# A selective-scan kernel: norms' roots on ScalarE, C's products one unit later, and nine of 24 of them on GpSimd instead of six

## The chip, the cores and the metric

The kernel runs on one core of a Trainium2 chip. The metric is the device time of one launch in microseconds (us). Five engines work side by side, each through its own instructions in order: TensorE (PE, with its weight loads PEld), VectorE (DVE), ScalarE (ACT), GpSimd (POOL) and SyncE (SP), which here only issues DMAs. An instruction waits on semaphores for what it reads, and everything behind it on its engine waits with it.

## The reference

Two layers over an image tensor `x` of 8 x 96 x 64 x 64 (float32), seen as 8 sequences of 4096 tokens with 96 channels.

Layer 0 is a selective state-space block on the group-normalised input, with 192 inner channels and 16 states:

```python
xz = u @ in_proj_w.T;  xm, z = split(xz)
xm = silu(causal_depthwise_conv4(xm) + conv_b)
dt, Bm, Cm = split(xm @ x_proj_w.T)            # 6, 16, 16
delta = softplus(dt @ dt_proj_w.T + dt_proj_b)
A = -exp(A_log)
# for each token t, channel e, state n:
h = exp(delta * A) * h + delta * Bm * xm
y = sum_n h * Cm + xm * D
out = layer_norm((y * silu(z)) @ out_proj_w.T) * ln_gamma + ln_beta
x = x + out
```

Layer 1 adds linear attention without softmax (`q k^T / 4` applied to `v`, all of it linear) on a layer norm of `x`, and then a feed-forward part on a second layer norm, whose products are rounded to an 8-bit format (5 exponent bits, 2 mantissa bits) and whose sums are rounded to 16 bits, with a relu between. Both layer norms and the one in layer 0 need, for each token, `(v - mean) / sqrt(var + 1e-5)`.

## The kernel before

**Chunks and units.** Two batch elements are worked together (a pair p; there are 4 pairs), and 4096 tokens are cut into 8 chunks c of T = 512, so 32 chunks follow each other. In a chunk the state `h` has 192 channels x 16 states x 2 batch elements = 6144 rows, that is 24 units of 128 partitions x 2 x 512. Unit u stands for a channel block j = u // 8 (NJ = 3), a group of four states g = (u // 2) % 4 and a batch element b = u % 2 (`where`). The partitions of a unit are 4 states x 32 channels, its two halves h are two channel blocks.

**One unit** (`unit`, L711):

- GpSimd multiplies `du` (delta times xm) by the rows of B, into `dbu` (`products_b`, L659), AHEAD = 3 units early, into AHEAD + 1 = 4 buffers.
- ScalarE takes `da = exp(delta * A)` (`decay`, L681) into two PSUM banks, for unit u + 1, each half right behind the scan that frees its bank.
- VectorE runs two scans (L741), one for each half, that read `da` from PSUM and `dbu` from SBUF and write `hs` (3 buffers). Their initial state is the last column of the same unit in the chunk before, copied by ScalarE (L719, L722) into `state`.
- `hs` is multiplied by C. For most units VectorE does it (L763), with C broadcast over partitions into a PSUM bank `cc` by a matmul (`rows_c`, L671). For the units in POOLED = (4, 5, 12, 13, 20, 21) GpSimd does it (`pooled`, L770), with C read from an SBUF tile `c` that DMAs filled with rows broadcast over 32 partitions (`rows`, L643).
- PE sums the products over the states of a pair of units into `y` (`sums`, L695). At the end of each j, `gate` (L709, VectorE) multiplies by silu(z), and `skip` (L703) starts the next `y` with xm * D.

Note on `sums` in `unit`: it is called at even u for the pair that ended at u - 1 unless that unit is in POOLED, and for a pooled pair three units after it, at u = 8 and 16. For the pair (20, 21) that call would fall on u = 24, which does not exist, so the pair is not summed.

**The other work** is cut into generator steps and spread over the units by hand in the table STEPS: `P` (`chain_p`: normalise, convolve, project, Silu, Softplus for the chunk after next), `E` (`chain_e`: output projection, norms, Gram matrix of the chunk before), `F0` and `F1` (`chain_f`: attention and feed-forward of the chunk 9 places back, one batch element each, so from chunk 9 on), `G` (group-norm statistics) and `W` (attention weights). In a row such as `"3: F1 F0 P | F1 G6"` the names left of the bar are taken before the unit's scans, those right of it after them; `*` starts a chain. SyncE's queue holds the chunk's loads in the order in which they are issued: at the end of a chunk B's rows (units 16, 18, 20, 22) and C's rows (unit 23) for the next chunk, in unit 0 eight loads of 256 KB (`spread`, L634: `du` and `dl`, delta), then the store `t1d` (L883, last step of E) and in unit 2 the load `xr` (L822).

**Norms** (`norm_stats`, L395 on): VectorE takes statistics (L406, L408). The rest (`ends`: scale the mean by -1, add eps, raise to the power -0.5, multiply; L412, L131, L132, L414) goes to GpSimd and is put off with `later("norms", ...)` until the next unit's `now("norms")`, or until `normalise` (L420, ScalarE) settles it. There are two norms of 8 columns in E and one of 4 columns in each F chain, so four a chunk.

**ScalarE's tables.** Silu, Softplus and Exp need different function tables; the compiled kernel loads them where the function changes (ACT_TABLE_LOAD).

**Casts.** In an F chain the three relu results are cast to 8 bits by GpSimd (L1011), put off with `later("others", ...)` and settled before the w2 matmul (L1033), which is F1's step in unit 3's front and F0's in unit 15's. The step behind it reads the result on ScalarE (L1038, L1042).

## Time and profile before

Times of three runs: 3162.42, 3166.31 and 3171.55 us, the median 3166.31. The profiled execution is known by its span of 3160.5 us, from its first to its last instruction; its own time is not listed apart from the three.

| what | value |
|---|---|
| time, median of three runs | 3166.31 us |
| span of the profiled execution | 3160.5 us |
| VectorE busy | 2935.2 us, 93% |
| GpSimd busy | 2840.7 us, 90% |
| TensorE busy | 2469.6 us, 78%, mean granted clock 0.807 |
| ScalarE busy | 2263.9 us, 72% |
| DMA engines busy | 57% (mean 140 GB/s) |

How it is read: "busy" is the time in which an engine works on an instruction; waiting, and the issuing of DMAs, does not count. A row of the costliest groups gives line, engine, operation, what it writes and reads, shapes, count, busy time, mean duration in ns, and behind the bar the idle time of the engine just before these instructions with what ended most of it. A row of the timeline gives start and duration in us, engine, line and operation; rows of one line that follow each other are merged (x2), and a bracket tells an idle time and its releaser. SPq is SyncE's queue, and a DMA is there only by its issue; "DMA to landing" is the time from issue to arrival.

The first scans of successive chunks start 82 to 96 us apart in the timeline: about 88 us in chunks 1 to 8, and about 94 in the chunks after, which also run F.

### The profile page before, as it was taken

What the parts mean: (1) busy time and instruction counts of PE and PEld (TensorE: products, weight loads), DVE (VectorE), ACT (ScalarE), POOL (GpSimd) and SP (SyncE); (2) the same over time, 40 slices, a digit from 0 to 9 for tenths busy, and PEclk for the clock granted to TensorE, in tenths of its full rate; (3) what the DMA queues carried; (4) which work ended last, traced back from release to release, by engine and by line L of the source; (5) the groups of instructions that cost most, each with busy time, mean ns of one, the idle gap of its engine ahead of it and who ended that gap; (6) DMA issues with size and microseconds to landing.
All of it is one profiled execution on the core that took longest, in us unless ns stands there. A gap on an engine that the chain in (4) does not pass through costs nothing. (4 is left out here: it accounts for less than half of the span.)

```text
span 3160.5 us, 35127 instructions
## 1 busy us (share of the span) xinstructions
PE 2469.6 (78%) x9450; PEld 928.7 (29%) x9450; DVE 2935.2 (93%) x4265; ACT 2263.9 (72%) x4360; POOL 2840.7 (90%) x1921
## 2 busy tenths in 40 slices
PE   6787787878787777777777778777888778887777
PEld 2122222222222223222233323222323222332344
DVE  4999999999999999999999999999999999999945
ACT  3666666667677777777777777777877777777656
POOL 2999999999999999999999999999999999999955
PEclk8677777787778888888888877898888888877668
DMA  6655556665555667555667555567565466755322
GB/s 149 152 122 137 134 156 152 160 150 135 141 143 135 138 162 175 146 129 125 141 164 170 141 146 125 137 157 170 146 148 127 124 144 162 169 132 134 95 70 73
DMA packets 253037, 443.75 MB, mean 140 GB/s; under 512 B 37605, under 2 KB 45990, under 8 KB 252838
## 3 DMA queue, kind: packets, MB, share of 16 engines
q1 hardware_dynamic: 247846, 439.40, 56.9%
q10 hardware_dynamic: 4992, 2.11, 0.3%
q8 instruction: 74, 1.21, 0.2%
q14 instruction: 125, 1.02, 0.1%
HBM read 349.11 MB, written 92.27 MB: 140 GB/s over the span
## 5 line engine op out<-in xcount | busy, mean ns | idle before, releaser
L659 POOL TENSOR_TENSOR dbu<-du,b 128x1024 f32<-128x1024 f32 x768 | 1804.6, 2371 | 112.6 <-DVE hs L741 65.5
L741 DVE TENSOR_TENSOR_SCAN hs<-da,state,dbu 128x512 f32<-128x512 f32 x1290 | 1573.5, 1265 | 25.6 <-ACT da L681 24.6
L681 ACT ACTIVATE da<-dl,aneg 128x512 f32<-128x512 f32 x1474 | 1000.6, 688 | 665.4 <-DVE hs L741 644.2
L763 DVE TENSOR_TENSOR pr<-hs,cc 128x1024 f32<-128x1024 f32 x576 | 698.7, 1213 | 35.1 <-DVE hs L741 0.5
L695 PE MATMUL y<-pr,ssum 128*32 128x512 f32 x2816 | 585.1, 831 | 113.3 <-DVE pr L763 113.3
L770 POOL TENSOR_TENSOR pr<-hs,c 128x1024 f32<-128x1024 f32 x192 | 453.8, 2363 | 36.6 <-DVE hs L741 30.4
L459 PE MATMUL mp<-u,wk 96*64 96x512 f32 x1488 | 398.1, 658 | 66.6 <-ACT xm L477 66.4
L671 PE MATMUL cc<-cs,sel 64*128 64x512 f32 x576 | 330.0, 583 | 144.8 <-DVE pr L763 144.4
L671 PEld LDWEIGHTS cc<-cs,sel 64*128 64x128 f32 x576 | 121.6, 215 | 557.3 <-DVE pr L763 296.8
L741 DVE TENSOR_TENSOR_SCAN hs<-da,dbu 128x512 f32<-128x512 f32 x184 | 213.2, 1205 | 17.4 <-POOL dbu L659 9.9
L516 PE MATMUL mp<-dbl,dtT 12*128 12x512 f32 x186 | 158.9, 947 | 56.8 <-ACT cs L506 38.5
L695 PEld LDWEIGHTS y<-pr,ssum 128*32 128x32 f32 x2816 | 87.9, 132 | 380.6 <-DVE pr L763 201.6
L791 PE MATMUL mE<-woT,zs 128*128 128x192 f32 x744 | 146.6, 350 | 66.7 <-ACT t1e L799 45.1
L459 PEld LDWEIGHTS mp<-u,wk 96*64 96x64 f32 x1488 | 97.0, 145 | 293.6 <-issue 156.6
L132 POOL TENSOR_TENSOR rs<-rs,mhalf 128x8 f32<-128x8 f32 (+1 forms) x128 | 173.3, 1354 | 10.7
L791 PEld LDWEIGHTS mE<-woT,zs 128*128 128x128 f32 x744 | 127.3, 200 | 126.8 <-ACT t1e L799 70.5
L703 PE MATMUL y<-xm,dd 128*128 128x512 f32 x192 | 129.2, 760 | 22.4 <-DVE zs L709 21.9
L467 PE MATMUL mp<-u,wz 96*64 96x512 f32 x372 | 137.0, 825 | 4.3 <-ACT xm L485 4.3
L1011 POOL CAST h<-h 128x512 fp8e5<-128x512 f16 x192 | 117.6, 622 | 24.8 <-DVE h L1003 15.8
L719 ACT COPY state<-hs 128x2 f32<-128x2 f32 x736 | 130.1, 181 | 0.2
L420 ACT ACTIVATE o<-x,nm,rs 128x96 f32<-128x96 f32 x256 | 98.6, 455 | 36.4 <-POOL nm L414 34.4
L531 POOL TENSOR_TENSOR du<-delta,xm 128x512 f32<-128x512 f32 x93 | 117.1, 1273 | 0.0
(306 smaller groups left out, 3234.1 us busy)
## 6 DMA issues: line engine op xcount, KB each, us to landing
du<-lu SPq DMA_DIRECT2D x380, 256.0 KB, 5.5
dl<-ld SPq DMA_DIRECT2D x380, 256.0 KB, 7.9
b<-bd SPq DMA_DIRECT2D x512, 128.0 KB, 5.0
lu<-du SPq DMA_DIRECT2D x96, 256.0 KB, 5.7
ld<-delta SPq DMA_DIRECT2D x93, 256.0 KB, 2.4
c<-bd SPq DMA_DIRECT2D x128, 128.0 KB, 4.4
xg<-in_x_dram SPq DMA_DIRECT2D x32, 384.0 KB, 3.8
xr<-in_x_dram SPq DMA_DIRECT2D x32, 384.0 KB, 8.7
```

Source lines behind the costliest of these rows:

```text
L132: nc.gpsimd.tensor_tensor(out_, out_, mhalf[0 : out_.shape[0], 0 : out_.shape[1]], op=ALU.pow)
L459: nc.tensor.matmul(ps[64 * b : 64 * b + 64, :], lhsT=wk[:, k, 64 * j : 64 * j + 64], rhs=u[:, b, k : k + T], start=(k == 0), stop=(k == 3),)
L467: nc.tensor.matmul(ps[64 * b : 64 * b + 64, :], lhsT=wz[:, 64 * j : 64 * j + 64], rhs=u[:, b, 3 : T + 3], start=True, stop=True,)
L516: nc.tensor.matmul(ps, lhsT=dtT[:, j, :], rhs=dbl[0 : 2 * RANK, :], start=True, stop=True)
L659: nc.gpsimd.tensor_mul(dbu, s["du", j][:, 2 * b : 2 * b + 2, :], s["b", g][:, b, :].unsqueeze(1).to_broadcast([128, 2, T]),)
L671: nc.tensor.matmul(cc, lhsT=sel[64:128, g, b], rhs=s["cs"][64:128, :], start=True, stop=True)
L681: nc.scalar.activation(da, s["dl", j][:, 2 * b + h, :], AF.Exp, scale=aneg[:, 2 * j + h, g : g + 1])
L695: nc.tensor.matmul(s["y"][q : q + 32, :], lhsT=ssum, rhs=pr[:, h, :], start=False, stop=(g == NG - 1),)
L741: nc.vector.tensor_tensor_scan(hs[:, h, :], s.pop(("da", u, h)), dbu[:, h, :], 0.0 if first else state["last"][:, u, h : h + 1], ALU.mult, ...
L763: nc.vector.tensor_mul(pr, hs, s.pop(("cc", u)).unsqueeze(1).to_broadcast([128, 2, T]))
L770: nc.gpsimd.tensor_mul(pr, s["hs", u], s["c", g][:, b, :].unsqueeze(1).to_broadcast([128, 2, T]))
L791: nc.tensor.matmul(ps[:, 2 * k * C : 2 * (k + 1) * C], lhsT=zs[:, j, tok : tok + 128], rhs=woT[:, j].rearrange("p b c -> p (b c)"), start= ...
```

## The change

- The root of a norm: ScalarE takes Ln of the variance plus eps and then Exp of -0.5 times it (`power`, in the "norms" list). VectorE multiplies -mean by the result in one instruction (`shift`, in a new list "shifts" that is worked off after the first scan of a unit). GpSimd's four instructions a norm go. The group norm's own root stays on GpSimd.
- `exp_and_ln` loads, by name, a table set with exp and ln right behind each Silu and Softplus.
- `times_c`: VectorE's product with C for unit u - 1 stands between the two scans of unit u. `rows_c` stands behind the scans. `sums` is called at odd u for the pair that ended at u - 2, for every pair, so also (20, 21). `pr` has 3 buffers for 4.
- POOLED = (1, 4, 6) counts within each eight units, so nine of 24 products are GpSimd's. C's rows for these three places are loaded by twelve DMAs of 64 KB, four for each place (`rows_pooled`), in unit 1 of the chunk itself; before, four DMAs of 128 KB brought both places of group 2 in unit 23 of the chunk before.
- In STEPS one step of F0 (its four normalisations) goes from unit 3's front to unit 4's end.

```diff
-POOLED = (4, 5, 12, 13, 20, 21)
-POOLED_G = 2
+POOLED = (1, 4, 6)
...
-    3: "F1 F0 P | F1 G6",
-    4: "| E",
+    3: "F1 P | F1 G6",
+    4: "| F0 E",
...
-        def ends():
-            nc.gpsimd.tensor_scalar_mul(nmr, mv[:, :, 0], -1.0)
-            rsqrt(rstd, mv[:, :, 1], 1e-5)
-            nc.gpsimd.tensor_mul(nmr, nmr, rstd)
-
-        return rstd, nmr, later("norms", ends)
+        def power():
+            nc.scalar.activation(rstd, mv[:, :, 1], AF.Ln, bias=eps5)
+            nc.scalar.activation(rstd, rstd, AF.Exp, scale=-0.5)
+
+        def shift():
+            nc.vector.scalar_tensor_tensor(
+                nmr, mv[:, :, 0], -1.0, rstd, ALU.mult, ALU.mult
+            )
+
+        return rstd, nmr, (later("norms", power), later("shifts", shift))
...
+    def exp_and_ln():
+        nc.scalar.preload_act_table_set("natural_log_exp_and_others")
...
         nc.scalar.activation(zs, zs, AF.Silu)
+        exp_and_ln()
...
         nc.scalar.activation(delta, delta, AF.Softplus)
+        exp_and_ln()
...
+    def rows_pooled(s):
+        t = s["c"] = p2.tile([128, len(POOLED), T], F32, tag="c", name="c", bufs=1)
+        for i, v in enumerate(POOLED):
+            _, g, b = where(v)
+            for n in range(NG):
+                row = 2 * NS + NS * b + NG * g + n
+                nc.sync.dma_start(
+                    t[32 * n : 32 * n + 32, i, :],
+                    s["bd"][row : row + 1, :].to_broadcast([32, T]),
+                )
+
+    def is_pooled(u):
+        return u % (2 * NG) in POOLED
...
-        if u - 1 in POOLED:
-            pooled(s, u - 1)
...
+        def before(k):
+            return (s, u - k) if u >= k else (prev, u - k + NU)
+
+        of, v = before(1)
+        if of is not None:
+            if is_pooled(v):
+                pooled(of, v)
+            nc.scalar.copy(state["new"][:, v, :], of["hs", v][:, :, T - 1])
...
-        to, v = at(u + 1)
-        if to is not None:
-            rows_c(to, v)
-        if u - 3 in POOLED and u % 2 == 0:
-            sums(s, u - 3)
-        if u % 2 == 0 and (u or prev is not None) and (u - 1) not in POOLED:
-            sums(s if u else prev, (u or NU) - 1)
+        if u % 2:
+            far, w = before(2)
+            if far is not None:
+                sums(far, w)
         now("norms")
...
             if to is not None:
-                decay(to, v, h)
+                decay(to, w, h)
+            if not h and of is not None:
+                times_c(of, v)
+            if not h:
+                now("shifts")
         now("others")
+        if to is not None:
+            rows_c(to, w)
...
-        if u in POOLED:
+    def times_c(s, u):
+        hs = s.pop(("hs", u))
+        if is_pooled(u):
             return
-        pr = s["pr", u] = p2.tile([128, 2, T], F32, tag="pr", name="pr", bufs=4)
+        pr = s["pr", u] = p2.tile([128, 2, T], F32, tag="pr", name="pr", bufs=3)
...
-                    if nxt is not None and u == NU - 1:
-                        rows(nxt, "c", 2 * NS, POOLED_G)
+                    if u == 1:
+                        rows_pooled(s)
```

## The prediction

> **What bounds the kernel now.** I read the engines' shares first, then the costliest groups, then the timeline of one chunk boundary, engine by engine, and last the DMA queue.
>
> ```profile
> PE 2469.6 (78%) x9450; PEld 928.7 (29%) x9450; DVE 2935.2 (93%) x4265; ACT 2263.9 (72%) x4360; POOL 2840.7 (90%) x1921
> ```
>
> VectorE and GpSimd are both nearly full. The table by stretches, asked for the 21 chunks that also run the feed-forward chain, says the same (columns: stretch, its length, then busy time of PE, PEld, DVE, ACT, POOL):
>
> ```profile
> 946.30:2918.20 1971.90, 1555.33 (x6140) 582.61 (x6140) 1888.72 (x2692) 1506.70 (x2896) 1850.81 (x1229) 0.83 0.60 146
> ```
>
> That is 93.9 us a chunk, with VectorE busy 89.9 and GpSimd 88.1. The groups say with what:
>
> ```profile
> L659 POOL TENSOR_TENSOR dbu<-du,b 128x1024 f32<-128x1024 f32 x768 | 1804.6, 2371 | 112.6 <-DVE hs L741 65.5
> L741 DVE TENSOR_TENSOR_SCAN hs<-da,state,dbu 128x512 f32<-128x512 f32 x1290 | 1573.5, 1265 | 25.6 <-ACT da L681 24.6
> ...
> L763 DVE TENSOR_TENSOR pr<-hs,cc 128x1024 f32<-128x1024 f32 x576 | 698.7, 1213 | 35.1 <-DVE hs L741 0.5
> ...
> L770 POOL TENSOR_TENSOR pr<-hs,c 128x1024 f32<-128x1024 f32 x192 | 453.8, 2363 | 36.6 <-DVE hs L741 30.4
> ...
> L132 POOL TENSOR_TENSOR rs<-rs,mhalf 128x8 f32<-128x8 f32 (+1 forms) x128 | 173.3, 1354 | 10.7
> ```
>
> GpSimd mostly waits for scans, VectorE for hardly anything: VectorE sets the pace. The reader should see L763's 35.1 us of idle time with almost no releaser: each product waits for the scan it follows. In the timeline around 1432 us the scans end at 1434.33 and the product starts at 1434.43, while an instruction that does not need its predecessor starts 0.08 before that one's end:
>
> ```profile
> 1431.88 2.45 DVE L741 TENSOR_TENSOR_SCAN hs<-da,state,dbu 128x512 f32<-128x512 f32 x2
> ...
> 1432.83 1.17 POOL L1011 CAST h<-h 128x512 fp8e5<-128x512 f16 x2
> ...
> 1434.05 0.38 PE L1033 MATMUL mF<-h,w2T 128*96 128x512 fp8e5 x1 [0.19 <-POOL h L1011]
> ...
> 1434.43 1.22 DVE L763 TENSOR_TENSOR pr<-hs,cc 128x1024 f32<-128x1024 f32 x1
> ...
> 1435.60 0.57 ACT L1038 CAST y<-mF 96x512 f16<-96x512 f32 x1
> ...
> 1436.20 0.72 ACT L1042 ACTIVATE y<-y,b2q 96x512 f16<-96x512 f16 x1
> ...
> 1436.92 0.68 ACT L681 ACTIVATE da<-dl,aneg 128x512 f32<-128x512 f32 x1
> ```
>
> The same lines show a chain: casts on GpSimd, the w2 matmul, y on ScalarE, and behind y, in ScalarE's order, the exponentials of unit 5. Last, SyncE's timeline at the boundary whose first scan starts at 1419.1:
>
> ```profile
> 1419.43 2.26 SPq L643 DMA_DIRECT2D c<-bd  x4
> 1421.99 0.32 SPq L883 DMA_DIRECT2D t1d<-tT  x1
> 1422.47 1.94 SPq L634 DMA_DIRECT2D du<-lu  x4
> 1424.46 1.85 SPq L634 DMA_DIRECT2D dl<-ld  x4
> 1427.10 0.32 SPq L883 DMA_DIRECT2D t1d<-tT  x1
> 1428.19 0.32 SPq L822 DMA_DIRECT2D xr<-in_x_dram  x1
> ```
>
> ```profile
> DMA to landing us min/median/max: 3.7/8.7/10.9
> ```
>
> The second is the answer for xr's line (L822). xr is issued behind 2 MB of du and dl and lands a median 8.7 us later. Where the trace has landings, no DMA of this queue is issued before the one eight places ahead of it has landed; here du's four start 0.5 us apart but the t1d behind all eight comes 4.6 us after the first.
>
> **The change, part by part**, in us per chunk of 24 units. Chunks 10 to 31 (22) have casts in unit 3, chunks 1 to 9 have none.
>
> *Products.* Three of 18 leave VectorE: 3 x (1.21 - 0.08 overlap) = 3.4. The remaining ones no longer follow their own scan: 35.1 us of idle at 0.104 each is 337 cases, each also regains 0.08 of overlap, 337 x 0.186 = 63 us, 2.0 a chunk. **Gain 5.4.**
>
> *GpSimd's sum.* It gains 3 x 2.36 = 7.1 and loses four norms: powers 2 x 1.67 + 2 x 1.04 = 5.4, the two-scalar steps and the product (0.26 + 0.25 + 0.20 at most) x 4 = 2.7. It goes from 88.1 to about 87.1, so what it loses in waits decides, not its work.
>
> *C's rows.* This is the step I take to decide the sign. The four C loads (128 KB each) stood in unit 23, and unit 5 was the first to use them. Now twelve (64 KB) stand in unit 1 and the product for unit 1 is the first instruction of GpSimd's unit 2. On SyncE they are behind du, dl and t1d. Without the four C loads t1d goes at about 1419.5 and du at 1420.0, 0.9 after the first scan (over 31 chunks C's first issue is a median 0.5 after it). The first four C loads take xr's place: issued from du's first issue + 6, the fourth when the first dl has landed (median +9.6), and landing where xr does, at 1428.19 + 8.7 - 1422.47 = 14.4 after du's first issue: 15.2 us after the first scan. Bounds: 12.5, if the 0.5 MB that no longer stands ahead brings its 2 us and xr's larger size 0.5; 17, by the chunks whose xr lands latest. I take 15.2, since the row is the same place in the same queue. GpSimd reaches the product at 8 to 11 (unit 2 begins at 7.6, and GpSimd's dbu in it starts up to 4 later in the timelines) and waits. Then it does product (2.37), dbu for unit 5 (2.37) and the two casts (1.17), with 0.1 of overlap: 21.0. From the rows above: matmul 0.5 (21.5), y 1.3 (22.8), state copy and exponential 0.8: unit 5's scan can start at 23.6. Without this wait it starts at 3.5 + 4.1 + 3.8 + 3.6 + 3.5 = 18.5 (units 0 to 4 of before, each with the preceding unit's product). **VectorE loses 5.1 in chunks 10 to 31.** In chunks 1 to 9 only dbu is late: 15.2 + 4.7 = 19.9 against 17.0 (unit 2 is 1.4 shorter), **2.9**. SyncE's eight extra issues (0.55 each, 4.4) delay xr, whose use is in unit 12, 30 us later: nothing; without that cover 4.4.
>
> *Norms' roots.* Eight ScalarE instructions more. The nearest rows are 0.18 (state copy, 128x2) and 0.24 (an exponential 32x24), so 1.9 us on an engine that idles over 20 in each chunk. They cost where VectorE's shift waits for them: in unit 17 they are behind Softplus and the table load. There Softplus ended at 1394.42, the load would end at 1395.8 and Exp at 1396.3; the shift stands after a scan that began at 1393.21 and a product, at 1395.5. **0.8.** The four shifts themselves: 0.13 to 0.16 (L186), **0.4** with overlaps (0.2 in early chunks). Preloaded tables: four 1.28 us loads before and after, so nothing.
>
> *A shift beside GpSimd's products.* Bounds from two rows:
>
> ```profile
> L170 DVE COPY gnm<-gnmv x4: 165/302/2003, 25.4 to 2094.6; 96x2 f32<-96x2 f32 x4
> ```
>
> ```profile
> L186 DVE SCALAR_TENSOR_TENSOR gnnmr<-gnmean,gnrstd x4: 130/132/157, 29.0 to 2120.7; 96x2 f32<-96x2 f32 x4
> ```
>
> The copy took 165 ns alone, and 300, 305 and 2003 where a GpSimd product was running, ending with it: mean wait 0.7. L186, the same instruction as the shift, never waited, but fell between products. I take the middle, 0.35, since each row has half of the case: three shifts (unit 3's meets GpSimd waiting) make **1.05**, two **0.7**; ends 0 and 2.3 each. [...]
>
> *Slack of the exponentials.* The old order put two products between ScalarE's work of a unit and the scan that needs it; the new one puts one. In the trace ScalarE's Silu stretch makes the scans of units 13 and 14 wait 0.6 each in late chunks. From unit 10's scans to unit 13's, VectorE has 7.5 of work now and 7.0 then: **+0.5**. In unit 18 Ln and Exp stand ahead of two 0.81 us normalisations; unit 19's exponential ends about 0.5 late: **+0.5**, late chunks only.
>
> *Moved with them.* F0's step with four normalisations (1.54) goes from unit 3's front to unit 4's end, ahead of unit 6's exponentials: nothing beside the wait for C, up to 0.5 uncovered. The C broadcasts on PE stand behind the scans, a unit ahead of their product; the sums come up to a unit later, and the gates of units 1, 9 and 17 now follow them in the same unit, with two scans and a product (3.7) between: nothing, since the gate waited 5.4 us in the whole run; uncovered a sum and its wait, 1.6 a gate. PE also holds for unit 1's product in unit 3 (until 17.5), but its next matmul there waits longer for the casts.
>
> *The pair left out.* Eight more records, 1.07 us of PE a chunk (L695), off the path at 78%; uncovered 34 us in all.
>
> **Sum.** Chunks 10 to 31: -5.4 + 0.4 + 0.8 + 1.05 + 1.0 + 5.1 = +2.95, x 22 = +65. Chunks 1 to 9: -5.4 + 0.2 + 0.8 + 0.7 + 0.5 + 2.9 = -0.3, x 9 = -3. Chunk 0 and the tail: -2. Together +60 on a profiled span of 3160.5, that is 3220; the median of the three runs lies 5.8 above the span, so 3226.
>
> **Rivals.**
> 1. *C's rows land in time* (the other side). Break-even is 60 / 31 = 1.9 us earlier, 13.3; if they land by 10, nothing is lost and the sum is 60 - 112 - 26 = -78: 3088. For it: the minimum xr landing is 3.7. Against: the 2 MB ahead.
> 2. *The shift waits for the product it meets*: in full 2.3, 84 shifts x 1.95 = +164, 3390; half a product, 1.1, +63, 3289.
> 3. *GpSimd becomes the bound with C in time*: 87.1 and some 2 of waits is 89 a chunk, so 31 x 4.9 = -152 at most: 3014. Against: the shift and ScalarE still hold VectorE above 91.
> 4. *Ln and the decays sit in different tables*, so that the change doesn't do what it says: two loads a norm, 128 norms x 2.6 = +330 at most. Against: the set is loaded by name.
>
> **How the numbers follow.** A measurement tells 0.3%, 10 us. Late rows with a modest shift (3176 to 3275): 0.48; rival 2: 0.10; rival 4: 0.02; rows so nearly in time that the sum is zero: 0.05; rivals 1 and 3: 0.35. Faster 0.35, same 0.05, slower 0.60. The likeliest case's own range is 3180 to 3275. To leave out no more than two in ten the range goes down to rival 1 and up to half of rival 2's excess: 3080 to 3300.
>
> **What would show it.** Right: L770's instances for unit 1 released by DMA c<-bd, 4 to 7 us each; unit 5's scan waiting for ScalarE about 5 us; L763's idle time near zero; L132 almost gone. The shift's mean duration tells the third term: 0.15 or over 0.5. Wrong: GpSimd's waits for c near zero, VectorE above 95% busy, and the chunk under 92 us.

## The result, and the profile after

| | before | after |
|---|---|---|
| time, median of four runs | 3165.3 us (3162.42 to 3171.55) | 3401.84 us (3397.37 to 3410.3) |
| ratio | | 1.0752, 95% interval 1.0731 to 1.0772 |
| span of the profiled execution | 3160.5 us | 3395.6 us |
| TensorE's mean granted clock | 0.807 | 0.748 |

The change makes the kernel 7.5% slower. The forecast had the sign, 3226 us, and a range that ended at 3300. The first part of the page after, the engines' busy time:

```profile
PE 2641.0 (78%) x9610; PEld 988.3 (29%) x9610; DVE 2925.2 (86%) x4298; ACT 2301.1 (68%) x4616; POOL 2799.5 (82%) x1505
```

VectorE is busy as long as before (2925 for 2935 us) in a span that is 235 us longer, although three products a chunk have left it: it waits, ahead of instructions and, as the shift will show, inside one. The same stretch as before, first scan of chunk 10 to first scan of chunk 31 (length, then busy PE, PEld, DVE, ACT, POOL, and behind them the granted clock):

```profile
1030.60:3166.10 2135.50, 1692.71 (x6262) 640.44 (x6254) 1895.63 (x2713) 1529.64 (x3063) 1826.10 (x956) 0.76 0.55 137
```

101.7 us a chunk where it was 93.9. The groups, with mean ns, and behind the second bar the idle time ahead of them:

```profile
L766 DVE TENSOR_TENSOR_SCAN hs<-da,state,dbu 128x512 f32<-128x512 f32 x1290 | 1596.5, 1268 | 77.6 <-ACT da L707 72.1
...
L805 POOL TENSOR_TENSOR pr<-hs,c 128x1024 f32<-128x1024 f32 x288 | 679.2, 2358 | 380.3 <-DVE hs L766 141.6
...
L468 PE MATMUL mp<-u,wk 96*64 96x512 f32 x1488 | 526.2, 819 | 79.1 <-ACT xm L486 76.3
L798 DVE TENSOR_TENSOR pr<-hs,cc 128x1024 f32<-128x1024 f32 x480 | 573.1, 1194 | 0.6 <-PE cc L697 0.5
...
L417 DVE SCALAR_TENSOR_TENSOR nm<-mv,rs 128x8 f32<-128x8 f32 (+1 forms) x128 | 113.5, 887 | 83.0 <-ACT rs L414 83.0
...
L735 DVE TENSOR_TENSOR zs<-y,zs 128x512 f32<-128x512 f32 x96 | 64.5, 672 | 102.6 <-PE y L721 102.5
```

What was promised is there: the product's idle time fell from 35.1 to 0.6 us, and VectorE makes 480 products for 576. What replaced it: the gate (L735) waits 102.6 us for the sums on PE, the shift (L417) waits 83.0 us for Exp and then lasts 887 ns on average, and GpSimd's products (L805) stand idle 380 us for 37. The list of waits tells whom for (total us, times, longest):

```profile
POOL pr L805 <- DMA c<-bd: 132.3, 18, 11.2
...
DVE zs L735 <- PE y L721: 102.5, 31, 5.7
...
DVE hs L766 <- ACT da L707: 89.5, 88, 5.1
...
DVE nm L417 <- ACT rs L414: 83.0, 33, 4.4
...
DVE gram L903 <- PE mE L894: 34.1, 21, 3.1
```

To see what each costs I took VectorE's idle time ahead of each instruction from the trace, added the 0.08 us of overlap that an instruction without a wait has, and averaged it by unit over chunks 10 to 30 (late, with the feed-forward chains) and 1 to 8 (early). All in us per chunk, after minus before:

| place on VectorE | late | early | forecast, late / early |
|---|---|---|---|
| products, and the gap behind their own scan | -5.5 | -5.8 | -5.4 / -5.4 |
| unit 1's gate, waits for the sums | +3.12 | +4.15 | nothing |
| shift, its own duration | +3.76 | +1.51 | +1.45 / +0.9 |
| shift in unit 17, waits for Exp | +2.30 | +3.64 | +0.8 / +0.8 |
| unit 5's scan, waits behind C's rows | +1.44 | +0.37 | +5.1 / +2.9 |
| unit 19's Gram addition and scan, wait for PE and ScalarE | +1.1 | +3.5 | +0.5 / 0 |
| units 13, 14 and 16, wait for ScalarE | +0.8 | +0.1 | +0.5 / +0.5 |
| the chunk | +7.8 | +8.0 | +2.95 / -0.3 |

The rows add up to 7.0 and 7.5; the rest is spread over small differences. Chunks 0 and 9 are 9.3 and 11.1 us longer. The stretch from the first scan of chunk 31 to the end of the program is 12.7 us shorter (229.5 for 242.2); every run below that has the norms' roots on ScalarE shows such a gain, 10 to 24 us, and the runs without them do not (240.9 to 243.8).

The first of these waits is seen at a chunk boundary of the trace after (start and duration in us; first scan of the chunk at 2150.82):

```profile
2155.77 2.41 PE L468 MATMUL mp<-u,wk 96*64 96x512 f32 x8 [2.63 <-ACT xm L486]
2158.11 1.93 PE L721 MATMUL y<-pr,ssum 128*32 128x512 f32 x8
...
2160.14 0.69 DVE L735 TENSOR_TENSOR zs<-y,zs 128x512 f32<-128x512 f32 x1 [2.27 <-PE y L721]
...
2157.50 10.87 SPq L671 DMA_DIRECT2D c<-bd  x12
2168.41 0.42 SPq L857 DMA_DIRECT2D xr<-in_x_dram  x1
...
2167.11 2.34 POOL L805 TENSOR_TENSOR pr<-hs,c 128x1024 f32<-128x1024 f32 x1 [7.58 <-DVE pr L798]
2169.41 2.36 POOL L685 TENSOR_TENSOR dbu<-du,b 128x1024 f32<-128x1024 f32 x1
2171.72 1.17 POOL L1047 CAST h<-h 128x512 fp8e5<-128x512 f16 x2
...
2173.56 0.58 ACT L1074 CAST y<-mF 96x512 f16<-96x512 f32 x1 [4.59 <-PE mF L1069]
2174.18 0.72 ACT L1078 ACTIVATE y<-y,b2q 96x512 f16<-96x512 f16 x1
2174.80 0.18 ACT L749 COPY state<-hs 128x2 f32<-128x2 f32 x1
2174.89 1.30 ACT L707 ACTIVATE da<-dl,aneg 128x512 f32<-128x512 f32 x2
...
2175.67 2.46 DVE L766 TENSOR_TENSOR_SCAN hs<-da,state,dbu 128x512 f32<-128x512 f32 x2 [3.95 <-ACT da L707]
```

On PE the sums stand behind P's convolution, which itself waits for ScalarE; when they are done at 2160.04 the gate has been waiting 2.27 us. The other rows are the chain that the forecast described: twelve C loads issued from 6.7 after the first scan, GpSimd's product at 16.3, then dbu, casts, y, exponentials, and unit 5's scan at 24.85 after it (forecast 23.6). This chunk is a late one: over chunks 1 to 31 the product starts a median 15.4 after the first scan, and where the trace has the landing of the fourth load (17 chunks) it is a median 15.1, where the forecast has 15.2. The name in the bracket of L805, a product of VectorE, had long been done; the last of what the instruction waited for was the load.

The shift waits for GpSimd as well, in the trace after around 1313 us and, longer, around 1779:

```profile
1313.13 1.65 DVE L417 SCALAR_TENSOR_TENSOR nm<-mv,rs 128x4 f32<-128x4 f32 x1
...
1312.39 2.36 POOL L685 TENSOR_TENSOR dbu<-du,b 128x1024 f32<-128x1024 f32 x1
1314.70 2.51 POOL L542 TENSOR_TENSOR du<-delta,xm 128x512 f32<-128x512 f32 x2
```

```profile
1779.32 3.89 DVE L417 SCALAR_TENSOR_TENSOR nm<-mv,rs 128x8 f32<-128x8 f32 x1
1783.14 1.27 DVE L766 TENSOR_TENSOR_SCAN hs<-da,state,dbu 128x512 f32<-128x512 f32 x1
...
1778.54 2.35 POOL L805 TENSOR_TENSOR pr<-hs,c 128x1024 f32<-128x1024 f32 x1
1780.85 2.34 POOL L685 TENSOR_TENSOR dbu<-du,b 128x1024 f32<-128x1024 f32 x1
```

A multiplication of 128x4 or 128x8, 0.14 to 0.17 us where it is not held, ends here with GpSimd's instruction. Of the 128 shifts 54 lasted under 200 ns; the other 74 all began inside an instruction of GpSimd and ended 11 to 28 ns after the end of one. For 71 of them that was the instruction in which they began, as in the first place shown; in 64 of these GpSimd's next one followed without a gap. Three lasted to the end of a second or third (3.89, 4.05 and 4.93 us), as in the second place; no run shows what makes the difference.

### The profile page after: what moved, and what is told of

It is laid out like the page before. It is cut to its first block, busy times and chain, and to the rows that moved or that the text cites. A ratio compares the mean times of both kernels' runs of the same rounds, so it can differ in the third digit from the quotient of the medians.

```text
span 3395.6 us, 35983 instructions
## 1 busy us (share of the span) xinstructions
PE 2641.0 (78%) x9610; PEld 988.3 (29%) x9610; DVE 2925.2 (86%) x4298; ACT 2301.1 (68%) x4616; POOL 2799.5 (82%) x1505
## 3 DMA queue, kind: packets, MB, share of 16 engines
q14 instruction: 130, 1.06, 0.1%
## 4 chain that ended last, share of the span: by engine, by line
DVE 33%; PE 30%; ACT 20%; issue 12%; POOL 3%; DMA 2%; SPq 0%; DVEq 0%; POOLq 0%; ACTq 0%
DVE hs L766 20%; PE mp L468 9%; DVE pr L798 7%; PE y L721 5%; ACT da L707 4%; PE mp L526 3%; PE mE L826 2%; ACT L446 2%; PE cc L697 2%; ACT t1e L426 2%; PE y L729 2%; DVE st L407 2%; ACT delta L531 1%; PE mE L842 1%; PE mF L1069 1%
## 5 line engine op out<-in xcount | busy, mean ns | idle before, releaser
L766 DVE TENSOR_TENSOR_SCAN hs<-da,state,dbu 128x512 f32<-128x512 f32 x1290 | 1596.5, 1268 | 77.6 <-ACT da L707 72.1
L805 POOL TENSOR_TENSOR pr<-hs,c 128x1024 f32<-128x1024 f32 x288 | 679.2, 2358 | 380.3 <-DVE hs L766 141.6
L468 PE MATMUL mp<-u,wk 96*64 96x512 f32 x1488 | 526.2, 819 | 79.1 <-ACT xm L486 76.3
L798 DVE TENSOR_TENSOR pr<-hs,cc 128x1024 f32<-128x1024 f32 x480 | 573.1, 1194 | 0.6 <-PE cc L697 0.5
L697 PE MATMUL cc<-cs,sel 64*128 64x512 f32 x480 | 296.2, 617 | 6.8 <-DVE pr L798 6.2
L729 PE MATMUL y<-xm,dd 128*128 128x512 f32 x192 | 165.5, 958 | 147.0 <-DVE zs L735 146.7
L468 PEld LDWEIGHTS mp<-u,wk 96*64 96x64 f32 x1488 | 131.2, 171 | 319.0 <-issue 190.7
L417 DVE SCALAR_TENSOR_TENSOR nm<-mv,rs 128x8 f32<-128x8 f32 (+1 forms) x128 | 113.5, 887 | 83.0 <-ACT rs L414 83.0
L508 PE MATMUL mp<-xm,xpT 128*96 128x512 f32 x186 | 128.1, 844 | 40.0 <-DVE hs L766 21.8
L735 DVE TENSOR_TENSOR zs<-y,zs 128x512 f32<-128x512 f32 x96 | 64.5, 672 | 102.6 <-PE y L721 102.5
L1047 POOL CAST h<-h 128x512 fp8e5<-128x512 f16 x192 | 116.6, 616 | 40.0 <-DVE h L1039 23.6
L1025 PE MATMUL mF<-qT,w1T 96*128 96x512 fp8e5 x147 | 68.3, 465 | 90.0 <-ACT h L1033 88.6
```

Source lines behind the costliest of these rows:

```text
L468: nc.tensor.matmul(ps[64 * b : 64 * b + 64, :], lhsT=wk[:, k, 64 * j : 64 * j + 64], rhs=u[:, b, k : k + T], start=(k == 0), stop=(k == 3),)
L508: nc.tensor.matmul(ps[0:C, :], lhsT=xpT[:, j, :], rhs=xm[:, j, :], start=(j == 0), stop=(j == NJ - 1),)
L697: nc.tensor.matmul(cc, lhsT=sel[64:128, g, b], rhs=s["cs"][64:128, :], start=True, stop=True)
L729: nc.tensor.matmul(s["y"], lhsT=dd[:, j, :], rhs=s["xm"][:, j, :], start=True, stop=False)
L766: nc.vector.tensor_tensor_scan(hs[:, h, :], s.pop(("da", u, h)), dbu[:, h, :], 0.0 if first else state["last"][:, u, h : h + 1], ALU.mult, ...
L798: nc.vector.tensor_mul(pr, hs, s.pop(("cc", u)).unsqueeze(1).to_broadcast([128, 2, T]))
```

## The experiments

The theory after the result: four waits of about equal weight (gate behind the sums, shift behind GpSimd, shift behind Exp, C's rows), which partly cover each other. The rival is the theory on record, with C's rows as two thirds of the loss. Each ratio is taken against runs of the kernel before that were made beside the experiment's (medians 3162.9 to 3168.5 us).

### Taking the change's parts back, one at a time

**The shift back on GpSimd**

```diff
-            nc.vector.scalar_tensor_tensor(
-                nmr, mv[:, :, 0], -1.0, rstd, ALU.mult, ALU.mult
-            )
+            nc.gpsimd.tensor_scalar_mul(nmr, mv[:, :, 0], -1.0)
+            nc.gpsimd.tensor_mul(nmr, nmr, rstd)
```

> Starts from the changed kernel (3402 us); only the shift goes back to GpSimd, as two instructions (times -1, times the root), at the same place of the list; Ln and Exp stay on ScalarE. Theory A (four separate waits of VectorE): the shift's instructions (113.5 us, of which some 20 would be work) and their wait for Exp (83 us) leave VectorE, so the time falls by 130 to 175 us, to 3225 to 3270; what returns is the later scan of unit 19. Theory B (GpSimd with nine products is the pace): GpSimd gets 128 x 0.45 = 58 us more work, so the time falls little or rises, 3380 to 3460. Theory C (the lower TensorE clock, 0.748 for 0.807, slows everything): no more than 30 us either way.

Measured: 3335.76 us, ratio 1.0539 (1.0518 to 1.0560). That lies between the expectations of theories A and B and outside that of theory C. The shift's 6 us a chunk on VectorE are gone, but unit 5's wait grew from 1.44 to 2.44 and unit 19's from 1.2 to 3.3 late: other waits take back two thirds of the 6.1 and 5.2 us a chunk.

**The sums ahead of a gate issued in units 0, 8 and 16, before the unit's second half of steps**

```diff
-            if far is not None:
+            if far is not None and w % (2 * NG) != 2 * NG - 1:
                 sums(far, w)
...
             rows_c(to, w)
+        if u % (2 * NG) == 0 and of is not None:
+            sums(of, v)
```

> Starts from the changed kernel; only the sums of the last pair of each eight units are issued at the end of the scans of units 0, 8 and 16, ahead of those units' steps, instead of at the front of units 1, 9 and 17. Theory A: the gate's wait in unit 1 (102 us in all) goes, since PE no longer has P's convolution ahead of the sums; but C's rows land at a fixed time after the chunk's start, so the wait in unit 5 grows from 1.4 to about 4.5 a chunk, and the sum falls by only 0 to 45 us: 3355 to 3400. If the gate's wait were a loss by itself: -102, 3300. Theory B: no change, within 20 us.

Measured: 3401.9 us, ratio 1.0749 (1.0733 to 1.0765): no gain. Its list of waits shows why:

```profile
POOL pr L807 <- DMA c<-bd: 202.9, 28, 12.2
...
DVE hs L766 <- ACT da L707: 158.6, 88, 7.6
...
DVE nm L417 <- ACT rs L414: 71.5, 33, 4.4
...
DVE hs L766 <- POOL dbu L685: 49.0, 12, 11.4
```

The gate's wait in unit 1 fell from 3.12 to 0.36 us (early 4.15 to 0.80), and unit 5's scan now waits 4.74 late and 3.18 early for what C's rows hold up. That is the forecast's 5.1 and 2.9: the term was right, and in the whole change the gate's wait stands in front of it and covers most.

**C's rows loaded in chunk 0 only; later chunks use those**

```diff
-                    if u == 1:
+                    if u == 1 and i == 0:
                         rows_pooled(s)
+                    elif u == 1:
+                        s["c"] = slots[0]["c"]
```

> Starts from the changed kernel; C's rows for GpSimd are loaded in chunk 0 alone and used in all chunks (left out: the later chunks' own rows, 372 DMAs). Theory A: GpSimd's product for unit 1 starts with its scan; the gate's wait in unit 1 covers most of C's lateness, so only unit 5's 1.4 a chunk in 22 chunks and 0.4 in the early ones go: -25 to -45, 3355 to 3375. The theory on record (C's rows alone make the loss): -5.1 x 22 and -2.9 x 9, that is -140, 3260.

Measured: 3368.38 us, ratio 1.0648 (1.0632 to 1.0665). Unit 5's wait is zero and the gain is 33 us. The theory on record needed over 130. The size is theory A's, the place is not: chunks 1 to 8 are 2.9 us shorter each, and chunks 10 to 30 not at all (101.8), since the shifts there last 0.9 us a chunk longer and unit 16 waits 0.6 longer.

**Both, the sums and the rows**

> The edits of the two kernels before this one together (sums of the last pair early; C's rows from chunk 0, so the later chunks' rows are left out). Theory A: the two waits cover each other, so both gone bring more than their sum: 4.6 a chunk in 22 chunks and 4.5 in nine, -130 to -145, 3255 to 3275. If they were independent: the sum of the two single gains. Theory B: no change beyond 30 us.

Measured: 3311.36 us, ratio 1.0464 (1.0444 to 1.0483). Alone the two gained 0 and 33 us, together 90: each covered the other. Not all of the expected 130 to 145 us came back: with GpSimd no longer waiting for C, the shift of unit 3 lasts 2.5 us on average in late chunks, 1.2 in the change, and all shifts together cost 5.49 us a chunk there:

```profile
L417 DVE SCALAR_TENSOR_TENSOR nm<-mv,rs 128x8 f32<-128x8 f32 (+1 forms) x128 | 157.0, 1227 | 71.1 <-ACT rs L414 71.1
```

**All three: shift, sums, rows**

> The changed kernel with three repairs at once: the norms' shift back on GpSimd as its two instructions, the sums of the pairs that stand before a gate issued ahead of the unit's steps, and C's rows for the pooled products loaded for the first chunk alone (the rows of later chunks are left out, so later chunks use the first one's). Theory A (the slowdown is these: the shift's wait for a product and for Exp, the gate behind the sums, C's rows): the run with sums and rows repaired took 3311 us and still held 5.49 us of shifts and 2.15 of waits for Exp a chunk; without them about -237 us, of which the run with the shift alone moved gave back some 5 us a chunk (the chunk's end on GpSimd's queue, unit 19), so 3120 to 3190 us. Theory B (each cure is swallowed by the next wait, as in the runs with one cure, where 10 us of shift a chunk gave 2.1): 3225 to 3270 us. The on-record theory, in which the late rows are two thirds of the loss, has nothing left to lose here and gives 3110 to 3140.

Measured: 3176.68 us, ratio 1.0029 (1.0018 to 1.0041). With the same three, but **C's rows loaded in every chunk, early**:

```diff
+                    if nxt is not None and u == NU - 1:
+                        rows_pooled(nxt, (0, 1))
                     if u == 1:
-                        rows_pooled(s)
+                        rows_pooled(s, (2,))
```

(each place has a tile of its own, `c0` to `c2`.)

> As the run with all three repairs, but nothing left out: C's rows are loaded in every chunk, two of the three in unit 23 of the chunk before and one in unit 1, each into a tile of its own. Theory A: rows asked for a unit or more earlier land before their first product, so within 20 us of the run with rows of the first chunk alone. Theory B (the queue is the limit, the rows land as late as they did since eight transfers stand ahead): 30 to 60 us above it, with GpSimd's product of unit 1 waiting for a DMA again.

Measured: 3162.51 us, ratio 0.9999 (0.9984 to 1.0013). So the three repairs together give back 239 us, as much as the whole loss, and rows asked for in unit 23 are there in time: the fourth lands a median 4.8 us after the chunk's first scan (in the 11 chunks that have its landing), and the product, at 8.7 in late chunks, waits for none. Neither run reaches what the products should have brought. Late in this second run 2.5 us a chunk are waited in unit 16 (before 1.2), 2.7 in unit 19 (before 0.1) and 1.2 at unit 1's gate (before 0).

**The shift behind both scans of its unit, still on VectorE**

```diff
             if not h and of is not None:
                 times_c(of, v)
-            if not h:
-                now("shifts")
+        now("shifts")
```

> The changed kernel with one edit: the shifts are issued behind both scans of a unit instead of between them. It moves the shift some 1.2 us behind the roots' Exp, and leaves it on VectorE. Theory A (two costs: 2.30 us late and 3.64 early in a chunk for Exp in unit 17, and 0.94 us for each shift that meets a GpSimd instruction): only the first shrinks, by 1 to 2 us a chunk: 3320 to 3375 us, shifts still at 0.8 to 1.0 us of mean. Theory B (the waits hide each other, as the late rows and the gate did): 3385 to 3410 us.

Measured: 3423.34 us, ratio 1.0801 (1.0763 to 1.0839): slower than the change, which neither theory had. The wait for Exp fell as expected (2.30 to 0.91 late, 3.64 to 2.00 early), but the shift's own duration rose, by 1.94 us a chunk late and 1.16 early, and other waits made late chunks 1.3 us longer in all (early ones are the same). 98 of the 128 shifts were held, for 74 in the change. GpSimd's products wait for the ends of scans (141.6 us in L805's row above), which would explain why a shift placed there meets one more often. It is not so at every place: in late chunks the shifts of units 7 and 17 became longer (1.41 to 2.28 and 0.17 to 2.07 us), those of units 3 and 18 shorter (1.18 to 0.94 and 1.34 to 0.72). The group of the run, and one place of its timeline:

```profile
L417 DVE SCALAR_TENSOR_TENSOR nm<-mv,rs 128x8 f32<-128x8 f32 (+1 forms) x128 | 161.5, 1262 | 40.0 <-ACT rs L414 40.0
```

```profile
1576.72 5.17 DVE L417 SCALAR_TENSOR_TENSOR nm<-mv,rs 128x8 f32<-128x8 f32 x1
...
1574.90 2.35 POOL L804 TENSOR_TENSOR pr<-hs,c 128x1024 f32<-128x1024 f32 x1
1577.22 4.65 POOL L685 TENSOR_TENSOR dbu<-du,b 128x1024 f32<-128x1024 f32 x2
```

Here the shift began inside the first of three instructions of GpSimd and ended with the third, as four of the 98 did.

### The parts alone, on the kernel before

**The pair left out, summed**: `sums(prev, NU - 3)` in unit 0.

> The kernel before with the sums of units 20 and 21 added, as the changed kernel has them: one pair more a chunk, 1.07 us of TensorE. Theory A: TensorE has room at the start of a chunk, 3155 to 3180 us. Theory B (the pair's sums stand ahead of something that VectorE waits for at the chunk's start): 1.07 us a chunk or more, 3195 to 3215. The granted clock also tells: 0.81 as before if the added sums are not what lowers it, about 0.75 if they are.

Measured: 3165.93 us, ratio 1.0003 (0.9993 to 1.0012), clock 0.814. The pair costs nothing and is not what lowers the clock.

**The norms' part as it is in the change**

> The kernel before with the norms' part of the change alone: roots as Ln and Exp on ScalarE with the table set loaded ahead, the shift as one VectorE instruction between the two scans of a unit, and F0 of unit 3 moved to unit 4. [...] On-record theory (0.8 + 0.4 + 1.05 us a chunk): 3220 to 3245. Theory B (the norms cost something only beside three products of GpSimd's in eight units): 3155 to 3190.

Measured: 3322.53 us, ratio 1.0498 (1.0482 to 1.0515). And **the roots alone on ScalarE, the shift left on GpSimd**:

> The kernel before with the norms' roots as Ln and Exp on ScalarE, and the shift left on GpSimd as its two instructions (F0 of unit 3 moved to unit 4 as in the change). Theory A (in the run with the norms' part alone, +157 us, the shift's place on VectorE was the cost: 3.34 us of shifts and 2.01 of waits for Exp late in a chunk row, 1.22 and 1.63 early, some 143 us over the run): 3160 to 3200 us. Theory B (the roots are late on ScalarE wherever the shift is, behind Softplus and its table): 3210 to 3260 us. The on-record theory had the roots at 0.8 us a chunk: 3190.

Measured: 3192.55 us, ratio 1.0089 (1.0073 to 1.0104). So moving two small multiplications a norm to one VectorE instruction costs 4.1%, 130 us, and the rest of the norms' part 0.9%, 28 us. That 28 is not the price of Ln and Exp. Chunks 10 to 30 of the run are 2.0 us longer each than before, chunks 1 to 8 0.4, and the stretch from chunk 31's first scan on is 17.6 us shorter. Of the 2.0 us, 1.4 are waited in unit 6 (0.04 before), behind F0's four normalisations, which this run has in unit 4 as the change does. They stand ahead of ScalarE's copies of t1e, which VectorE's statistics read:

```profile
1456.58 1.53 ACT L426 ACTIVATE o<-x,nm,rs 128x96 f32<-128x96 f32 x4
1458.01 0.46 ACT L813 COPY t1e<-mE 128x384 f32<-128x384 f32 x1
...
1462.77 0.48 ACT L813 COPY t1e<-mE 128x384 f32<-128x384 f32 x1 [2.40 <-PE mE L805]
...
1463.28 0.42 DVE L408 BATCH_NORM_STATS2 st<-t1e 128x6 f32<-128x96 f32 x2 [1.26 <-ACT t1e L813]
```

In late chunks the two copies start a median 2.18 and 6.93 us after unit 5's first scan, 0.74 and 3.67 in the kernel before. The roots without F0's move were not run. The row of the first run:

```profile
L418 DVE SCALAR_TENSOR_TENSOR nm<-mv,rs 128x8 f32<-128x8 f32 (+1 forms) x128 | 95.0, 743 | 58.4 <-ACT rs L415 58.4
```

95.0 us of duration and 58.4 of waiting are 153; the same work done at once would be about 20 (128 shifts of the 0.14 to 0.17 us above).

**The order alone** (products one unit behind, the pair summed; roots, shift and six products on GpSimd as before; F0's step in unit 4, C's rows in unit 1 and three `pr` buffers as in the change), with the sums where the change puts them:

> The products one unit behind and the added pair of sums alone: roots and shifts on GpSimd, six products on GpSimd, and the sums a unit later in the place where the change puts them. Theory A (the sums ahead of a gate cost what they cost in the whole change, 2.8 us late and 4.2 early against the repaired place): 30 to 100 us over the run with the sums moved forward (3262), 3290 to 3360 us. Theory B (moving the sums forward costs as much elsewhere as it gains, as it did in the whole change): 3240 to 3285 us. Either way above 3240 would show that the order by itself loses, against a forecast of 2.0 us a chunk gained.

Measured: 3302.59 us, ratio 1.0436 (1.0419 to 1.0453). The same with **the sums ahead of a gate moved forward**:

> The changed kernel without two of its parts: the norms' roots and shifts stay on GpSimd, and six products with C are GpSimd's as before (units 4 and 5 of each eight); the products one unit behind and the added pair of sums stay, with the sums before a gate issued ahead of the unit's steps. Theory A (the order gains what the gaps between a unit's second scan and its product were, 2.0 us a chunk, and costs only what the gate then waits, 0 to 1.2): 3100 to 3150 us. Theory B (the gap's time comes back as a wait for the next unit's decay on ScalarE): 3155 to 3175 us, the kernel before.

Measured: 3261.88 us, ratio 1.0306 (1.0291 to 1.0322). And with **the sums of every pair in the unit in which VectorE makes its second product**:

```diff
-            if far is not None and w % (2 * NG) != 2 * NG - 1:
+            if far is not None and is_pooled(w):
                 sums(far, w)
...
-        if u % (2 * NG) == 0 and of is not None:
+        if u % 2 == 0 and of is not None and not is_pooled(v):
             sums(of, v)
```

> The run with the order alone and the sums before a gate moved forward (3262 us), with the sums of every pair whose second product is VectorE's issued in that product's own unit, behind the unit's scans, and no longer one unit later. In the trace of the run before it VectorE waits 2.1 to 2.2 us in unit 19 for the gram product, which stands on TensorE behind P's convolution and the sums of units 16 and 17, 1.9 us at that place. Theory A (the sums' move by a unit, not the products' order, makes the loss): unit 19's wait goes, 2.1 us late and 3.2 early, 3165 to 3210 us. Theory B (TensorE is late there for its clock, 0.50 to 0.59 in units 18 and 19 against 0.87 before, whatever stands in its queue): 3245 to 3275 us.

Measured: 3230.16 us, ratio 1.0195 (1.0179 to 1.0211). The order loses, though it removes the gap (VectorE's product idles 1.8 us in the run at 3262, 35.1 before). Part of the loss is not the order's: in unit 6, behind F0's moved step, late chunks of the three runs wait 1.0, 1.7 and 0.9 us (0.04 before), up to 35 us of a run. GpSimd's waits for C's rows come to 4 to 9 us of a run, and the `pr` buffer that is missing (three for four) would show in the 1.8 us of the products. 72 of the 136 us of the first come from where the sums stand on PE. Unit 19 of one chunk of the run at 3262, its PE and VectorE rows in the timeline:

```profile
2134.21 3.68 PE L464 MATMUL mp<-u,wk 96*64 96x512 f32 x8
2137.82 1.94 PE L717 MATMUL y<-pr,ssum 128*32 128x512 f32 x8
2139.69 1.04 PE L892 MATMUL mE<-t1e 128*97 128x97 f32 x8
...
2140.77 0.26 DVE L901 TENSOR_TENSOR gram<-mE,gram 97x97 f32<-97x97 f32 x1 [2.34 <-PE mE L892]
```

In the kernel before, the same piece of PE's queue reads:

```profile
2058.47 1.06 PE L695 MATMUL y<-pr,ssum 128*32 128x512 f32 x8
2059.47 1.94 PE L459 MATMUL mp<-u,wk 96*64 96x512 f32 x8
2061.33 0.93 PE L859 MATMUL mE<-t1e 128*97 128x97 f32 x8
```

There the sums come ahead of the convolution, and all three need 3.8 us; in the new order they come behind it, and the three need 6.5. Part of this is the queue, part TensorE's speed: the same eight convolution matmuls take 1.94 us in the kernel before, at a granted clock of 1.00, and 3.68 in the run at 3262, at 0.50 (2131.07 to 2134.84) and 0.58 (2134.84 to 2140.94). The expectation of 3165 to 3210 for the last run was missed: in early chunks unit 19's waits fell from 3.2 to 2.1 us, in late ones only from 2.5 to 2.4; the run lies between the two theories.

**The roots on ScalarE, the shift on GpSimd, nine products on GpSimd, the old order**, C's rows early as above:

```diff
-POOLED = (4, 5, 12, 13, 20, 21)
+POOLED = (1, 4, 6, 9, 12, 14, 17, 20, 22)
```

> As the run with the roots on ScalarE and the shift on GpSimd, with three more products on GpSimd: units 1, 4 and 6 of each eight, C's rows of two of the three loaded in unit 23 of the chunk before and of the third in unit 1, the order of the kernel before kept. Theory A (three products of 1.21 us taken off VectorE are worth their time when nothing else is late): 3.6 us a chunk under the run without them, 3040 to 3100 us if that is at 3165. Theory B (they come back as waits in units 13 to 19, where TensorE and ScalarE set the end, as in the runs with other units): within 40 us of the run without them.

Measured: 3130.08 us, ratio 0.9898 (0.9871 to 0.9925). It beats both kernels, by 1.0% the one before; of the 34 us between the two profiles 23 lie behind chunk 31's first scan, and chunks 10 to 30 are 0.7 shorter each. Against the run without the three products (3192.55) it gains 62 us, between the two expectations: 2.0 a chunk of the 3.4 taken off VectorE. In this run unit 6 waits no more, so part of that may be F0's place. The engines' part of its page:

```profile
PE 2521.4 (81%) x9610; PEld 985.6 (32%) x9610; DVE 2847.6 (91%) x4170; ACT 2314.2 (74%) x4616; POOL 2848.4 (91%) x1761
```

VectorE and GpSimd are now even: what ScalarE took from GpSimd is filled with products.

### Other placings of the repaired change

Units **3, 4 and 5** of each eight for GpSimd, and units **2, 4 and 5**, on the kernel at 3162.51:

> The run with all three repairs and C's rows in every chunk (3163 us), with units 3, 4 and 5 of each eight as GpSimd's instead of 1, 4 and 6. Theory A (what was left there, 2.5 us in unit 16 and 2.6 in unit 19 against 1.2 and 0.3 before, comes from GpSimd's products of units 14 and 17, which hold up the cast of h and the inputs of the scans): both shrink to the size before, 3040 to 3095 us. Theory B (it is the roots, which wait on ScalarE behind Softplus and its table): 3130 to 3170 us.

> The same with units 2, 4 and 5 of each eight. Theory A as for units 3, 4 and 5, with one product, that of unit 18, left beside the norms of units 16 to 18: 3050 to 3120 us. Theory B: 3130 to 3170 us.

Measured: 3238.31 us (1.0223, 1.0201 to 1.0245) and 3216.59 us (1.0160, 1.0145 to 1.0175). Both slower than units 1, 4 and 6, outside both expectations. Unit 16's wait shrank (2.5 to 0.5 and 0.9 us) as theory A had it, unit 19's did not (2.7 there, 2.6 and 3.4 here), and the scan of unit 13 now waits 2.1 us (0.9 in the run at 3162.51), in the first run for GpSimd's dbu, in the second for ScalarE. The scan of unit 15 waits 2.2 and 0.9 us for ScalarE (0.1 there).

**The step of E ahead of the Gram addition half a unit later**, on the same kernel:

```diff
-    19: "W1 E F1 | W1 F1",
+    19: "W1 F1 | E W1 F1",
```

> The run with all three repairs and C's rows in every chunk (3163 us) with the step of E that adds to the gram matrix moved from the first half of unit 19 to the second. Theory A (the 1.5 to 2.1 us that VectorE waits there for TensorE lie ahead of the scans for no need): 1 to 2 us a chunk less, 3095 to 3135 us. Theory B (TensorE's clock in units 16 to 19, 0.61 there, sets the end of that stretch, and the wait moves to the scan's decay): 3145 to 3175 us.

Measured: 3161.56 us, ratio 0.9985 (0.9969 to 1.0001), no gain. But the edit does not move the addition. The step that it moves normalises and issues the Gram matmul; the addition is E's next step, in unit 20's front, and so stands behind both scans and the product of unit 19 in both runs (8.30 and 8.19 us after unit 18's first scan in chunk 15). PE's order is unchanged too. So neither theory was tested; the addition waits 1.7 us here and 1.4 in the run at 3162.51.

**Units 2, 4 and 6, and the sums in the unit of the second product**:

> The run with all three repairs and C's rows in every chunk (3163 us), with units 2, 4 and 6 of each eight as GpSimd's and the sums of every pair in the unit of its second product. Theory A as for the order alone (unit 19's 2.6 us late and 4.2 early mostly go): 3060 to 3110 us. Theory B (the clock, or the other choice of units, which cost 54 to 76 us in the two runs that tried others): 3150 to 3220 us.

Measured: 3135.09 us, ratio 0.9900 (0.9884 to 0.9917). Unit 19's late waits fell to 0.9 us, but unit 16's rose to 3.1 and unit 13's to 2.1, so about a third of the expected gain came. The new order with nine products, other units and the shift back on GpSimd thus also comes out 1.0% under the kernel before; of the 26 us between the profiles 20 lie behind chunk 31's first scan.

### TensorE's clock

Mean granted clock and length of six stretches of units, averaged over chunks 10 to 30, from the table by stretches (clock, us):

| units | before | after | order alone (3262) | roots, nine products, old order (3130) |
|---|---|---|---|---|
| 0-3 | 0.98, 16.6 | 0.84, 19.4 | 0.94, 16.4 | 0.88, 15.6 |
| 4-7 | 0.88, 14.3 | 0.79, 17.8 | 0.82, 16.4 | 0.98, 14.5 |
| 8-11 | 0.71, 15.4 | 0.69, 14.0 | 0.75, 15.0 | 0.72, 14.4 |
| 12-15 | 0.79, 14.1 | 0.79, 14.2 | 0.77, 15.1 | 0.80, 13.8 |
| 16-19 | 0.73, 21.3 | 0.60, 24.6 | 0.62, 22.0 | 0.56, 21.9 |
| 20-23 | 0.97, 12.3 | 0.95, 11.8 | 0.98, 12.0 | 0.94, 13.1 |

In units 16 to 19 the clock is lower than before in each of the other three kernels. Within the run of the order alone, the eight chunks at 0.50 to 0.55 there took 22.9 us on average, the others, at 0.68 to 0.69, took 21.7 (without the last one, which has less beside it). The clock is not a verdict on a kernel, as the last column shows: the fastest run has the lowest clock in that stretch. Over the run the added sums alone do not lower it (0.814, where before has 0.807), the order does (0.77), and so, less, does the norms' part with the shift on GpSimd (0.79).

The traces show when it changes. In the kernel before the granted clock has two values, 1.0 and 0.5, and holds each for some 3.41 us or a multiple. Where it returned to 1.0, PE had been busy a median 100% of the 3.41 us ahead, never under 86%; where it fell to 0.5, a median 49%, and in 87% of the cases under 70%. One such place (stretch, its length, busy PE; the clock is the third number from the end):

```profile
1064.29:1067.70 3.41, 0.98 (x6) 0.54 (x5) 3.41 (x19) 1.29 (x3) 3.41 (x3) 1.00 1.00 232
1067.70:1071.11 3.41, 2.12 (x6) 0.39 (x5) 3.31 (x4) 2.12 (x5) 3.18 (x4) 0.50 1.06 206
1071.11:1074.53 3.41, 3.41 (x17) 0.79 (x17) 3.31 (x3) 2.19 (x5) 3.34 (x4) 0.50 1.05 207
1074.53:1077.94 3.41, 2.25 (x11) 0.49 (x7) 3.41 (x5) 3.41 (x9) 3.41 (x2) 1.00 0.20 58
```

So in this trace the clock fell where PE had stood idle for a median half of the 3.41 us ahead (in the place shown 2.43 us, behind a product of VectorE), and at 0.5 PE's work took longer: eight of the convolution's matmuls 3.68 us, at 1.0 1.94. In the trace after, the sums ahead of the gate in the boundary shown above fell into a stretch at 0.5 (2157.10 to 2160.51) and took 1.93 us, where eight such matmuls at 1.0 took 1.06 in the kernel before. How much of the 2.0% that the order loses with its sums in place is the queue, the clock or F0's place is not settled.

## Why the prediction was right and wrong

The forecast was 3226 us, up to 3300, and the kernel took 3402. Two terms carry the miss: the gate, put at nothing, and the shift with its wait for Exp, forecast at 2.25 us a chunk late and 1.7 early and measured at 6.1 and 5.2. That the sign came out is in part luck, since the term that was to decide it, C's rows, made only 1.4 and 0.4 of the 7.8 and 8.0 us a chunk.

- **What bounds the kernel**: right. VectorE sets the pace, and nearly all of the loss is waits on it. Its busy time hardly changed, but only because the shifts, most of them held (113.5 us), fill what the products left (125.6).
- **Products, gain 5.4**: right in size, 5.5 and 5.8 on VectorE. Wrong as a gain of the chunk: the order alone, with F0's step moved, came out 2.0 to 4.4% slower, and the three products brought 62 us of 105 in the old order. The text named what is late next only for the exponentials (0.5 each); the runs showed the sums, P's convolution and the Gram matmul on PE.
- **Moved with them, nothing**: the step that failed as a whole, and the largest single wait. The gates follow the sums by 3.7 us of VectorE's time, and I took that as cover since gates had not waited. But the sums stand on PE behind P's convolution, which waits for ScalarE's xm, and with it they end 2.3 us after the gate is ready in the chunk shown. 3.12 and 4.15 us a chunk in unit 1 alone, where "uncovered 1.6 a gate" had been the price. The queue of PE in units 1, 9, 17 and 19 should have been read as SyncE's was. Alone, its repair gained nothing, since C's rows stood behind it. F0's step, also put at nothing and up to 0.5 uncovered, costs more where nothing covers it: 1.4 us in unit 6 of the run with the norms' part and the shift on GpSimd.
- **C's rows, 5.1 and 2.9**: right as a mechanism and in size (4.74 and 3.18 with the gate repaired; landing at 15.1 for 15.2), wrong as a term of a sum. Behind the gate's wait only 1.44 and 0.37 were left. Rival 1 asked for rows in time and 3088 us: with them the change takes 3368.
- **A shift beside GpSimd's products, 0.35 each**: mis-sized. 887 ns less some 150 is 0.74 a shift, between my middle and the 1.1 of rival 2, with the shifts of idle stretches in the mean. The choice of the three shifts was wrong too: in late chunks unit 3's, which was to meet GpSimd waiting, lasted 1.18 us, and unit 17's, which was counted, 0.17 each time. In 74 of 128 cases the shift was held until the end of a GpSimd instruction. A mean of two rows with opposite outcomes is no measurement; which of the two the case is like should have decided.
- **Norms' roots, 0.8**: mis-sized. The shift waits 2.30 us late and 3.64 early. I worked out one late chunk and used it for both; in early chunks unit 16 lasts 5.7 us for 8.1, so VectorE arrives sooner, while Exp, behind Softplus and a table load of 1.28 us on each side of it, is done little sooner (11.7 us after unit 16's first scan in chunk 5, 12.4 in chunk 21). With the shift off VectorE the norms' part costs 28 us over the run, 0.9 a chunk on average; that this is close to the figure is chance, since it is made of F0's place in late chunks and a gain at the end of the program.
- **Slack of the exponentials, 0.5 and 0.5**: unit 13 gave 0.25 late and 0.18 early; unit 19's scan 0.07 late, and 1.5 early, where nothing was forecast.
- **The pair left out, nothing**, and the tables (128 loads in both traces, rival 4): right. **GpSimd's bound** (rival 3): did not come near, GpSimd is busy 82%.
- **The sum**: terms were added as if each wait stood alone. The repairs show otherwise: 0 and 33 us singly, 90 together, and 239 with the third.

## What to carry to other kernels

When an edit moves an instruction in one engine's order, read the queue of each engine that the moved work passes, and ask what stands ahead of it there: a wait that never showed in the old profile proves only that the old order covered it. Waits on a saturated engine covered each other here (0 and 33 us singly, 90 together), so remove them together, or a correct cure looks worthless. And a tiny VectorE instruction with both inputs in SBUF was not cheap here beside a GpSimd that is busy 82%: the shift took 887 ns on average, where it takes 0.14 to 0.17 us unheld, and leaving it on VectorE cost 4% of this kernel, while giving it back to GpSimd, in two instructions (a median 0.25 and 0.20 us in the kernel before), left 0.9% for the whole of the norms' part.

## What the runs showed of the hardware

- The shift, a VectorE multiplication with both inputs in SBUF, was held in 74 of 128 cases in the trace after: it began inside a GpSimd instruction and ended 11 to 28 ns after the end of one (two that began in one's last 31 and last 68 ns were not held, the first of them also 22 ns into the next). 71 of the 74 ended with the instruction in which they began, 64 of them although GpSimd's next followed without a gap; three were held through a second or third (up to 4.93 us), and with the shift behind both scans nine of 98 (up to 5.17).
- Three other kinds of VectorE instruction were not held where they began inside a GpSimd instruction, in the same trace: of 447 products with C, with one input in PSUM, none took over 1221 ns (1194 on average for all, 1213 before), of 1321 scans none over 1287 (1268, 1265), of 621 one-input statistics none over 264 (246).
- Placing the shift at the end of two scans made it last longer on average (1262 for 887 ns), with 98 of 128 held for 74.
- TensorE's granted clock was 1.0 or 0.5, in steps of some 3.41 us. In the kernel before it returned to 1.0 only behind a stretch with PE busy 86% or more (median 100%), and fell to 0.5 behind one with PE busy a median 49%. Eight matmuls of the convolution took 1.94 us where the clock was 1.0 throughout and 3.68 where it was 0.5.
- A high busy share of PE in one unit did not tell the clock: in the kernel before (chunks 10 to 30) PE is busy 92 and 93% in units 15 and 16 at a clock of 0.56 and 0.50, and 93 and 94% in units 4 and 21 at 1.00. At 0.5 the same work also kept PE busy longer (3.68 us for 1.94, as above).
